# A perceiver layer on one core: the span attention's minimum taken a half batch later, and a product with the values moved within odd half batches

## The chip, the cores and the metric

The kernel runs on one core of a Trainium2 chip. The metric is the time of one execution on the device in microseconds, given as the median of several runs; one further execution was profiled, and what is said of engines, waits and single instructions comes from that one. A core has five engines that run side by side, each through its own list of instructions in a fixed order: TensorE (PE; matrix products and transposes, results in PSUM), VectorE (DVE), ScalarE (ACT), GpSimd (POOL) and SyncE (SP), which here issues most of the transfers (three early ones are ScalarE's). An engine waits at an instruction until the semaphores that the instruction names have been raised; everything behind it in its list waits too.

## What is computed

A perceiver layer in float32: cross attention from 64 latent rows to 1601 context rows for each of 32 batches, a self attention whose weights come from a learnt span, and a shared and a hashed mixture of feed-forward nets. Cut to what matters:

```python
x = x + xattn(layernorm(x), ctx, ctx)          # 16 heads of 16, 64 x 1601 scores a head
x = x + span_attention(layernorm(x))
x = x + ffn(layernorm(x))                      # shared silu net + two hashed experts

def span_attention(h):                         # per head: two numbers a row
    span, value = heads(h @ W_span.T), heads(h @ W_val.T)
    mean, soft = sigmoid(span[..., 0]) * m, softplus(span[..., 1])
    scores = -soft * (pos - mean) ** 2         # 64 x 64 per head
    return (softmax(scores) @ value) @ W_out.T
```

## The kernel before

**Half batches and stretches.** The main loop (L763) runs over 64 half batches: n = 2b + c, with b the batch and c the half of the heads. In step n it makes the scores of half batch n + 1, the softmax of n and the products with the values of n - 1, and it projects the context of batch b + 1: keys (`project_keys`, four pieces) and values (`project_values`, units 0 to 6 of two blocks of 124 rows each; units 0 to 2 in even steps, 3 to 6 in odd ones). A step has three stretches, one for each call of `scores`. The order on every engine is the order of the calls, written out by hand.

**One step, in TensorE's order (PE):** the first product with the values of n - 1 (`values(n - 1, 0)`, L633, into `pvs`); the scores of stretch 0 (L546, four PSUM tiles `psc`); the transposes `pm` of the row maxima of n (L594, they read `mx`); key piece 0; the transposes `pb` that spread the maxima back (L609); the span steps that are due (`run(3n)`); the second product `values(n - 1, 1)`; the scores of stretch 1 (L546, five blocks a row, so five `psc` tiles and a spare one); key piece 1; two value units; the steps of stretch 1; the scores of stretch 2; key pieces 2 and 3 and the rest of the value units, in four column tiles each (`tiled`); the steps of stretch 2.

**The other engines.** VectorE adds the mask to each score tile on its way to SBUF (`prob`, L570; the fifth blocks in L563), keeps a running maximum in PSUM (`mrun`, L587) and at the end of the step writes `mx`; the maxima after `pm` are reduced to `mc` (L601). ScalarE copies the projections out of PSUM (L507 keys, L524 values), copies the maxima `mb` (L613), begins a running maximum with a copy (L579) and does the softmax exponentials, four a step (L623). GpSimd subtracts the maxima from the scores, four times a step (L618). In even steps `finish_steps` on VectorE (L708 to L716) divides the products of the batch before by their sums.

**The span steps.** After every second batch, one tile t of 128 rows (two batches) is finished: the output projection of the cross attention and then the span attention, as a generator `span_steps` with 23 steps. A table says in which stretch, counted from the step in which the tile becomes ready (n = 4t + 4), each step runs: `STEPS` for tiles 0 to 12, and a table each for the last three. Since a tile takes four half batches, steps of two or three tiles are under way at a time. The steps, by the index of the table: 0 `po` (PE, L248), the residual add (DVE, L251) and the statistics; 1 and 2 the spread (POOL) and the normalisation (ACT, L214); 3 the transposes `tr_h` (PE) and the copy `hT` (ACT, L260); 4 `psp` (PE); 5 an exponential; 6 a chain of small VectorE operations (L291 to L303); 7 `pos - mean` (POOL, L308); 8 the square (ACT, L312) and the product with `soft` (POOL, L313); 9 the minimum `least` (DVE, L316); 10 to 13 four exponentials each (ACT, L320), which take `least` as their bias; 14 the reciprocal of the totals (DVE, L325); 15 the product with it (POOL, L327); 16 `pval` (PE, L336) and its copies to `vbd`; 17 the transposes `psa` (PE, L354) and copies `aT`; 18 to 22 the products `po` (L364 and L374), the second residual add (L377) with statistics, normalisation and the transposes `tr_f` whose copies (L387) feed the feed-forward nets. A second generator, `query_steps`, makes the queries of a later tile (`tr_q`, `xnT`, `pq`, `qbd`) from odd steps on.

**PSUM.** All of `psc`, `pk`, `pv`, `pm`, `pb`, `po`, `tr_h`, `psa` and the like take the next of six banks (`mm_bank`, tag `mm`); one more holds `pvs` with the spare score tile, and one `mrun`. A product into a bank waits until what the bank held has been read. So the order of the calls also settles which copy or add each product waits for.

**Wherever a step's list has several entries,** they run in the order in which they were put on the list: an entry goes there when its step before has run.

**The tail.** After the last step of the loop the last half batch is finished, the steps of the last tiles run in stretches 1 to 21 after `3 * last`, and between them stand the units of the shared feed-forward net (`unit`, `gate`; L662 on PE, L684 to L690 on ACT and DVE). Then come the experts (L905 on).

Of the kernel before, what the change touches and what calls it, by code (L numbers as in the profile page):

```python
# [18 lines left out]
ALU = mybir.AluOpType  # L19
# [70 lines left out]
def perceiver_kernel(ctx: ExitStack, tc: tile.TileContext, a: dict[str, bass.AP], out: bass.AP):  # L90
    nc = tc.nc
# [125 lines left out]
    def transposed(src, name: str):  # L217
# [10 lines left out]

    STEPS = (3, 4, 5, 6, 7, 8, 9, 10, 11, 12, 13, 14, 15, 16, 18, 19, 20, 21, 23, 24, 25, 26, 27)
    LAST_BUT_TWO = (
        3, 4, 5, 6, 7, 8, 9, 10, 11, 12, 12, 13, 14, 15, 16, 17, 17, 18, 20, 21, 22, 23, 24,
    )
    LAST_BUT_ONE = (2, 2, 3, 4, 5, 5, 6, 7, 8, 9, 10, 10, 10, 10, 11, 11, 12, 13, 14, 15, 15, 16, 17)
    LAST = (2, 2, 3, 4, 5, 6, 8, 9, 10, 11, 12, 12, 12, 12, 13, 13, 14, 15, 16, 17, 17, 18, 19)
    SMALL = 6

    def steps_of(t: int):
# [2 lines left out]
    def span_steps(t: int, oT):  # L242
        at = steps_of(t)
        waits = iter([b - a for a, b in zip(at, at[1:])])
# [61 lines left out]
        full = [P, H, S]  # L306
        sc = span_pool.tile(full, F32, tag="sc", name=f"sc_{t}")
# [7 lines left out]
        least, total = small("least"), small("total")  # L315
        nc.vector.tensor_reduce(least, sc, AX.X, ALU.min)  # L316
        yield next(waits)
        for part in range(4):
# [3 lines left out]
                    accum_out=total[:, h : h + 1],  # L322
                )
            yield next(waits)
        nc.vector.reciprocal(total, total)  # L325
        yield next(waits)
        nc.gpsimd.tensor_tensor(sc, sc, total[:, :, None].to_broadcast(full), ALU.mult)  # L327
        yield next(waits)


        pval = mm_bank(f"pval_{t}")
# [10 lines left out]
        for e in range(2):  # L342
            nc.scalar.copy(
                vbd[e * S : (e + 1) * S, :, e * DK : (e + 1) * DK],
                pval[e * S : (e + 1) * S, : 2 * P].rearrange("p (n d) -> p n d", d=DK),
            )
        yield next(waits)
        scf = sc.rearrange("p h k -> p (h k)")
        aT = span_pool.tile([P, NPAIR, P], F32, tag="aT", name=f"aT_{t}")
        for q in range(2):  # L350
            ps = mm_bank(f"psa_{t}_{q}")
            for i in range(4):
                n = 4 * q + i
# [175 lines left out]
    def scores(n: int, g: int, then=None, order=None):  # L529

        b, c = halves[n]
        c0, nb = SCORED[g]


        more = [mm_bank(f"psc_{b}_{c}_{g}"), spare_pvs] if nb == 5 else None
        pss = [mm_bank(f"psc_{b}_{c}_{g}_{j}") for j in range(4)]
        for r in range(nb):
            for j in range(4):
                e, s = divmod(j, 2)[::-1]
                fifth = nb == 5 and r == 4 * s  # L540
                i = 4 if fifth else r - (nb == 5 and s == 0)
                ps, at = (more[e], s) if fifth else (pss[j], i)
                if fifth and j == 2:
                    tc.add_manual_dep(nc.tensor.nop().ins, mm.ins.name, IN_TURN, reason="banks")
                k0 = (c0 + i) * CHUNK
                product = nc.tensor.matmul(  # L546
                    ps[:CHUNK, at * P : (at + 1) * P],
                    lhsT=kTs[c][32 * j : 32 * j + 32, k0 : k0 + CHUNK],
                    rhs=qbd[b // 2][32 * j : 32 * j + 32, c, b % 2, :, :],
                    start=True, stop=True, tile_position=(32 * j, 0),  # L550
                )
                if fifth and j == 1:
                    mm = product
        held = then() if then else None
        for item in (order or ORDER[g]).split():
            if item == "t":
                if held is not None:
                    maxima_of_rows(*held)
            elif item[0] == "m":
                maximum(n, int(item[1:]))  # L560
            elif item in "AB":
                k, e = c0 + 4, "AB".index(item)
                nc.vector.tensor_tensor(  # L563
                    block_of(n, k)[:, :, e, :],
                    more[e][:CHUNK, : 2 * P].rearrange("p (r q) -> p r q", r=2),
                    madd_fifth[:CHUNK, None, :].to_broadcast([CHUNK, 2, P]), ALU.add,
                )
            else:
                j = int(item)
                nc.vector.tensor_tensor(  # L570
                    pair_of(n, j)[:, c0 : c0 + 4, :].rearrange("p k (e q) -> p k e q", e=2),
                    pss[j][:CHUNK].rearrange("p (k e q) -> p k e q", k=4, e=2),
                    madd[:CHUNK, c0 : c0 + 4, None, :].to_broadcast([CHUNK, 4, 2, S]), ALU.add,
                )
# [3 lines left out]
    def first_maxima(n: int):  # L578
        nc.scalar.copy(mrun[:CHUNK].rearrange("p (r i) q -> p r i q", r=2), block_of(n, 0))  # L579
# [45 lines left out]
    def values(n: int, r: int):  # L625

        b, c = halves[n]
        v = vs[b % 2]
        for k in range(NKC):
            kn = min(CHUNK, KEYS - k * CHUNK)  # L630
            for j in range(4):
                h = 4 * r + j
                nc.tensor.matmul(  # L633
                    pvs[32 * j : 32 * j + DK + 1, c, :, r, :],
                    lhsT=v[:kn, k, 8 * c + h, :],
                    rhs=pair_of(n, h // 2)[:kn, k, (h % 2) * S : (h % 2) * S + S],
                    start=(k == 0), stop=(k == NKC - 1), tile_position=(0, 32 * j),
                )
# [56 lines left out]
    def run(stretch: int):  # L695
        for steps in agenda.pop(stretch, []):
            while (wait := next(steps, None)) == 0:
                pass
            if wait:
                agenda[stretch + wait].append(steps)  # L700

    def finish_steps(b: int, stretch: int):

        t = b // 2
        if b % 2 == 0:
            oT[t] = work.tile([P, 2, 2, S], F32, tag="oT", name=f"oT_{t}")
        flat = "p c u r q -> p (c u r q)"
        nc.vector.transpose(turned_pvs.rearrange(flat), pvs.rearrange(flat))  # L708
        by_head = turned_pvs.rearrange("p c u r i -> p (c u r) i")
        rec = work.tile([P, 8], F32, tag="rec", name=f"rec_{b}")  # L710
        nc.vector.reciprocal(rec, by_head[:, :, DK])
        o = work.tile([P, 8, DK], F32, tag="o", name=f"o_{b}")
        nc.vector.tensor_tensor(
            o, by_head[:, :, :DK], rec[:, :, None].to_broadcast([P, 8, DK]), ALU.mult
        )
        nc.vector.transpose(oT[t][:, :, b % 2, :], o.rearrange("p (c n) i -> p c (n i)", c=2))  # L716
        if b % 2:
            at = steps_of(t)
            agenda[stretch - 1 + at[0]].append(span_steps(t, oT.pop(t)))
            held_at.add(stretch - 1 + at[SMALL])  # L720
        yield
# [41 lines left out]
    for n, (b, c) in enumerate(halves[:-1]):  # L763
        if c == 0 and b + 1 < B:
            load_context(b + 1)
        if c and b % 2 == 0 and b // 2 + 1 < NTILE:
            agenda[3 * n].append(query_steps(b // 2 + 1))

        def project(f, *args):
            if b + 1 < B:  # L770
                f(b + 1, *args)

        def steps(g: int):
            run(3 * n + g)
            for u in extra.get(3 * n + g, ()):
                linear_factor(u)

        def taken_off():
            turned.extend(turned_maxima(n))
            return turned  # L780

        turned: list = []
        if n:
            values(n - 1, 0)
            exponentials(n - 1, 3)
        scores(n + 1, 0, taken_off)
        project(project_keys, c, 0)
        m = maxima_along_rows(turned[1])
        less_maxima(n, 0, m, nc.gpsimd)
        held = 3 * n in held_at  # L790
        if not held:
            first_maxima(n + 1)
        run(3 * n)
        if n:
            values(n - 1, 1)
            if c == 0:
                agenda[3 * n + 1].append(finish_steps(b - 1, 3 * n + 1))
        for u in extra.get(3 * n, ()):
            linear_factor(u)
        if held:  # L800
            first_maxima(n + 1)
        else:
            for k in (1, 2):
                maximum(n + 1, k)

        scores(n + 1, 1, order=LATER if held else None)
        exponentials(n, 0)
        project(project_keys, c, 1)
        for u in (4, 5) if c else (0, 1):
            project(project_values, u)  # L810
        less_maxima(n, 1, m, nc.gpsimd)
        steps(1)
        exponentials(n, 1)

        less_maxima(n, 2, m, nc.gpsimd)
        scores(n + 1, 2)
        project(project_keys, c, 2, True)
        project(project_keys, c, 3, True)
        for u in (3, 6) if c else (2,):
            project(project_values, u, True)  # L820
        less_maxima(n, 3, m, nc.gpsimd)
        exponentials(n, 2)
        steps(2)
# [176 lines left out]
```

## Time and profile before

| | |
|---|---|
| median of 3 runs | 1527.41 us (1525.89 to 1528.43) |
| the profiled execution: time, span | 1530.65 us, 1528.8 us |
| busy, share of the span: PE, DVE, ACT, POOL | 96%, 80%, 62%, 73% |
| granted TensorE clock, mean | 0.992 |
| mean DMA rate | 48 GB/s |
| `least` (L316), one | 1.10 to 1.19 us |
| an exponential of L320, one (x256) | 342 ns |
| L618 (GpSimd), one (x252) | 3753 ns |

Times in the lines of the profile are microseconds from the start of the span unless marked ns. A line of a timeline has the start, the time of the instruction or of several like it, the engine, the line of the code, the operation, what it writes and reads, and in brackets how long the engine stood idle before it and what ended that. A line of the chain of waits has the start, the time and the instruction; "issue" is time in which the profile shows nothing that was waited for. A PE that is busy is not a PE at its peak, since products are pipelined.

### The profile page before, as it was taken

What the parts mean: (1) busy time and instruction counts of PE and PEld (TensorE: products, weight loads), DVE (VectorE), ACT (ScalarE), POOL (GpSimd) and SP (SyncE); (2) the same over time, 40 slices, a digit from 0 to 9 for tenths busy, and PEclk for the clock granted to TensorE, in tenths of its full rate; (3) what the DMA queues carried; (4) which work ended last, traced back from release to release, by engine and by line L of the source; (5) the groups of instructions that cost most, each with busy time, mean ns of one, the idle gap of its engine ahead of it and who ended that gap; (6) DMA issues with size and microseconds to landing.
All of it is one profiled execution on the core that took longest, in us unless ns stands there. A gap on an engine that the chain in (4) does not pass through costs nothing.

```text
span 1528.8 us, 62985 instructions
## 1 busy us (share of the span) xinstructions
PE 1469.1 (96%) x28600; PEld 1069.2 (70%) x28600; DVE 1224.9 (80%) x2332; ACT 947.6 (62%) x1725; POOL 1121.4 (73%) x508
## 2 busy tenths in 40 slices
PE   8999999999999999999999999999999999988999
PEld 5677767677776767776767767676777777654587
DVE  4889898989888898989898888988898888873100
ACT  3565667666767666666757676666766676756311
POOL 1777788888787878888887878777888778852700
PEclk9999999999999999999999999999999999999899
DMA  5111111111111101111111111011111111005100
GB/s 173 44 37 46 46 46 46 50 38 49 49 49 50 45 25 40 53 46 44 44 50 49 50 49 46 23 42 53 37 51 46 49 46 36 3 6 159 59 28 28
DMA packets 52076, 73.82 MB, mean 48 GB/s; under 512 B 3812, under 2 KB 51040, under 8 KB 51680
## 3 DMA queue, kind: packets, MB, share of 16 engines
q1 hardware_dynamic: 50992, 69.00, 14.8%
q8 instruction: 225, 3.69, 1.0%
q10 hardware_dynamic: 816, 0.79, 0.2%
q14 instruction: 43, 0.35, 0.1%
HBM read 65.57 MB, written 4.19 MB: 46 GB/s over the span
## 4 chain that ended last, share of the span: by engine, by line
PE 77%; DVE 18%; ACT 2%; issue 2%; DMA 0%; POOL 0%; ACTq 0%; POOLq 0%; DVEq 0%
PE pk L492 20%; PE pv L492 18%; PE psc L546 11%; PE pvs L633 10%; DVE mrun L587 8%; DVE prob L570 5%; PE py L930 4%; PE pm L594 2%; PE u L662 2%; PE pb L609 2%; PE ph L912 2%; DVE least L316 1%; PE pq L463 1%; PE psa L354 1%; PE po L248 1%
## 5 line engine op out<-in xcount | busy, mean ns | idle before, releaser
L618 POOL TENSOR_TENSOR prob<-prob,mb 124x1664 f32<-124x1664 f32 x252 | 939.5, 3753 | 222.3 <-ACT mb L613 189.0
L570 DVE TENSOR_TENSOR prob<-psc,madd 124x512 f32<-124x512 f32 x768 | 506.2, 680 | 67.9 <-PE psc L546 66.7
L587 DVE TENSOR_TENSOR mrun<-prob,mrun 124x512 f32<-124x512 f32 x704 | 486.5, 691 | 28.3 <-ACT mrun L579 15.5
L623 ACT ACTIVATE prob<-prob 124x1664 f32<-124x1664 f32 x256 | 406.8, 1590 | 143.2 <-POOL prob L618 140.6
L492 PE MATMUL pk<-ct,wkT_sb 128*32 128x372 f32 (+1 forms) x2512 | 388.6, 490 | 5.6 <-DMA wkT_sb<-in_wkT 5.5
L492 PE MATMUL pv<-wvT_sb,ct 128*124 128x256 f32 x3524 | 380.9, 379 | 0.1
L492 PEld LDWEIGHTS pv<-wvT_sb,ct 128*124 128x124 f32 x3524 | 273.0, 132 | 108.8 <-issue 11.6
L546 PE MATMUL psc<-qbd,kT 32*124 32x128 f32 x6400 | 243.6, 280 | 10.7 <-issue 8.4
L492 PEld LDWEIGHTS pk<-ct,wkT_sb 128*32 128x32 f32 (+1 forms) x2512 | 149.2, 127 | 137.0 <-issue 92.7
L546 PEld LDWEIGHTS psc<-qbd,kT 32*124 32x124 f32 x6400 | 203.1, 181 | 49.1 <-issue 27.4
L524 ACT COPY v<-pv 124x512 f32<-124x512 f32 (+1 forms) x224 | 124.6, 557 | 181.9 <-PE pv L492 181.9
L633 PE MATMUL pvs<-prob,v 124*17 124x64 f32 x13312 | 212.7, 220 | 2.7 <-issue 2.7
L633 PEld LDWEIGHTS pvs<-prob,v 124*17 124x17 f32 x13312 | 195.4, 98 | 24.4 <-issue 16.5
L507 ACT ACTIVATE kT<-pk,cols 128x372 f32<-128x372 f32 (+2 forms) x256 | 148.0, 589 | 87.9 <-PE pk L492 87.7
L320 ACT ACTIVATE sc<-sc,least 128x64 f32<-128x64 f32 x256 | 85.8, 342 | 3.2 <-DVE least L316 3.2
L932 DVE SCALAR_TENSOR_TENSOR ot<-py,prob 128x256 f32<-128x256 f32 x16 | 6.8, 424 | 75.7 <-PE py L930 66.1
L594 PE MATMUL pm<-cst,mx 124*128 124x124 f32 x256 | 42.2, 285 | 22.7 <-DVE mx L587 18.9
L662 PE MATMUL u<-xfT,sw_sb 128*128 128x512 f32 x128 | 59.7, 615 | 0.9 <-ACT xfT L387 0.9
L579 ACT COPY mrun<-prob 124x512 f32<-124x512 f32 x64 | 38.4, 599 | 29.4 <-DVE soft L303 26.4
L546 PE MATMUL pvs<-qbd,kT 32*124 32x128 f32 x256 | 55.1, 294 | 0.0
L609 PEld LDWEIGHTS pb<-cst,mc 128*124 128x124 f32 x256 | 29.0, 135 | 37.3 <-DVE mc L601 29.0
L563 DVE TENSOR_TENSOR prob<-psc,madd_fifth 124x256 f32<-124x256 f32 x64 | 27.0, 422 | 32.2 <-PE pvs L546 29.1
(125 smaller groups left out, 1246.7 us busy)
## 6 DMA issues: line engine op xcount, KB each, us to landing
ct<-in_ctxT SPq DMA_DIRECT2D x64, 372.0 KB, 3.2
ct<-in_ctxT SPq DMA_DIRECT2D x32, 496.0 KB, 5.1
ct<-in_ctxT SPq DMA_DIRECT2D x32, 361.0 KB, 3.9
w<-in_w SPq DMA_DIRECT2D x16, 256.0 KB, 7.7
x<-in_x SPq DMA_DIRECT2D x16, 128.0 KB, 2.3
x_kept<-x SPq DMA_DIRECT2D x16, 128.0 KB, 2.3
prob<-x_kept SPq DMA_DIRECT2D x8, 256.0 KB, 5.3
out<-ot SPq DMA_DIRECT2D x16, 128.0 KB, 1.9
```

Of the source, the lines that this page charges most:

```text
L320: nc.scalar.activation(sc[:, h, :], sc[:, h, :], AF.Exp, bias=least[:, h : h + 1], scale=-1.0, accum_out=total[:, h : h + 1],)
L492: nc.tensor.matmul(out[at:end], lhsT=lhsT[:, at:end], rhs=rhs, start=start, stop=stop, **(dict(tile_position=(0, at)) if tiled else {}),)
L507: nc.scalar.activation(kTs[c][:, k0 : k0 + kn], ps[:, :kn], AF.Identity, bias=cols[:, B_K + c : B_K + c + 1])
L524: nc.scalar.copy(vs[b % 2][:kn, 2 * u : 2 * u + n, :, :DK], ps[:kn, : n * D].rearrange("p (n h d) -> p n h d", n=n, d=DK),)
L546: product = nc.tensor.matmul(ps[:CHUNK, at * P : (at + 1) * P], lhsT=kTs[c][32 * j : 32 * j + 32, k0 : k0 + CHUNK], rhs=qbd[b // 2][32 * j ...
L570: nc.vector.tensor_tensor(pair_of(n, j)[:, c0 : c0 + 4, :].rearrange("p k (e q) -> p k e q", e=2), pss[j][:CHUNK].rearrange("p (k e q) -> ...
L587: nc.vector.tensor_tensor(dst, block_of(n, k), run, ALU.max)
L594: nc.tensor.transpose(ps[:, j * CHUNK : (j + 1) * CHUNK], m[:CHUNK, j, :], ident[:CHUNK, :CHUNK])
L618: engine.tensor_tensor(sj, sj, m[:CHUNK, j, None, :].to_broadcast([CHUNK, NKC, P]), ALU.subtract)
L623: nc.scalar.activation(pair_of(n, j), pair_of(n, j), AF.Exp)
L633: nc.tensor.matmul(pvs[32 * j : 32 * j + DK + 1, c, :, r, :], lhsT=v[:kn, k, 8 * c + h, :], rhs=pair_of(n, h // 2)[:kn, k, (h % 2) * S : ( ...
L662: nc.tensor.matmul(ps, lhsT=w[:, c, hc * P : (hc + 1) * P], rhs=xfT[:, c, :, slot], start=(c == 0), stop=(c == 1),)
```

## The change

Three things change. The table `STEPS` puts the steps from 7 on later: `pos - mean` from 10 to 11, the square and product from 11 to 12, `least` from 12 to 15, the four groups of exponentials from 13 to 16 to 16 to 19; the tables of the last three tiles are changed too. In `span_steps` the step with `pval` now comes before the reciprocal and the product with it, which take its places 15 and 16 in the table. And in odd half batches value unit 3 is projected in stretch 0, ahead of the steps due there and in whole products instead of column tiles, while `values(n - 1, 1)` is moved from stretch 0 to stretch 2, after the scores there.

```diff
-    STEPS = (3, 4, 5, 6, 7, 8, 9, 10, 11, 12, 13, 14, 15, 16, 18, 19, 20, 21, 23, 24, 25, 26, 27)
+    STEPS = (3, 4, 5, 6, 7, 8, 9, 11, 12, 15, 16, 17, 18, 19, 20, 20, 21, 22, 23, 24, 25, 26, 27)
     LAST_BUT_TWO = (
-        3, 4, 5, 6, 7, 8, 9, 10, 11, 12, 12, 13, 14, 15, 16, 17, 17, 18, 20, 21, 22, 23, 24,
+        3, 4, 5, 6, 7, 8, 9, 11, 12, 13, 13, 14, 15, 16, 17, 17, 17, 18, 20, 21, 22, 25, 27,
     )
-    LAST_BUT_ONE = (2, 2, 3, 4, 5, 5, 6, 7, 8, 9, 10, 10, 10, 10, 11, 11, 12, 13, 14, 15, 15, 16, 17)
-    LAST = (2, 2, 3, 4, 5, 6, 8, 9, 10, 11, 12, 12, 12, 12, 13, 13, 14, 15, 16, 17, 17, 18, 19)
+    LAST_BUT_ONE = (
+        2, 2, 3, 4, 5, 5, 6, 7, 8, 9, 10, 11, 12, 13, 14, 14, 14, 15, 16, 17, 17, 18, 19,
+    )
+    LAST = (2, 2, 3, 4, 5, 6, 8, 9, 10, 11, 12, 12, 12, 12, 13, 13, 13, 15, 16, 17, 17, 18, 19)
...
             yield next(waits)
-        nc.vector.reciprocal(total, total)
-        yield next(waits)
-        nc.gpsimd.tensor_tensor(sc, sc, total[:, :, None].to_broadcast(full), ALU.mult)
-        yield next(waits)
         pval = mm_bank(f"pval_{t}")
...
         yield next(waits)
+        nc.vector.reciprocal(total, total)
+        yield next(waits)
+        nc.gpsimd.tensor_tensor(sc, sc, total[:, :, None].to_broadcast(full), ALU.mult)
+        yield next(waits)
...
         if not held:
             first_maxima(n + 1)
+        if c:
+            project(project_values, 3)
         run(3 * n)
-        if n:
+        if n and c == 0:
             values(n - 1, 1)
-            if c == 0:
-                agenda[3 * n + 1].append(finish_steps(b - 1, 3 * n + 1))
+            agenda[3 * n + 1].append(finish_steps(b - 1, 3 * n + 1))
...
         scores(n + 1, 2)
+        if c:
+            values(n - 1, 1)
         project(project_keys, c, 2, True)
         project(project_keys, c, 3, True)
-        for u in (3, 6) if c else (2,):
-            project(project_values, u, True)
+        project(project_values, 6 if c else 2, True)
```

## The prediction

> Half batches are q0, q1, q2, q3 by n mod 4 (c is odd in q1 and q3); V0 and V1 are the two products with the values, S0, S1, S2 the scores of the three stretches, line numbers those of the kernel before. I read the page's chain first, then the chain in detail over the four half batches from 785 to 870 us, then each engine's timeline there, and last the order and the semaphores of the changed kernel as built.
>
> **What bounds the kernel now.** The chain is TensorE's, with VectorE for 18% of the span:
>
> ```profile
> PE 77%; DVE 18%; ACT 2%; issue 2%; DMA 0%; POOL 0%; ACTq 0%; POOLq 0%; DVEq 0%
> ```
>
> In detail (start, us, what) it leaves TensorE once in four half batches, in q0:
>
> ```profile
> 789.38 0.43 DVE x L377
> ...
> 790.48 1.10 DVE least L316
> 791.58 0.61 DVE mrun L587
> ...
> 805.69 0.70 DVE mx L587
> 806.38 0.04 issue
> 806.43 0.64 PE pm L594 x4
> ```
>
> From the residual add at 789.38 VectorE never rests until mx, and TensorE's transposes pm of the next half batch (q1) wait for it. TensorE's timeline gives the wait:
>
> ```profile
> 806.43 0.64 PE L594 MATMUL pm<-cst,mx 124*128 124x124 f32 x4 [1.36 <-DVE mx L587]
> 829.37 0.38 PE L221 MATMUL tr_h<-cst,xn_h 128*128 128x128 f32 x2
> 829.90 1.65 PE L633 MATMUL pvs<-prob,v 124*17 124x64 f32 x104
> 831.47 0.37 PE L546 MATMUL psc<-qbd,kT 32*124 32x128 f32 x1
> ```
>
> In the steady part the q1, q2 and q3 half batches begin pm without such a wait; pm to pm they take 20.35, 21.05 and 20.59 us of TensorE alone, q0 20.70 with 1.36 of waiting. VectorE's and ScalarE's timelines show how much room the others have:
>
> ```profile
> 790.39 1.19 DVE L316 TENSOR_REDUCE least<-sc 128x16 f32<-128x1024 f32 x1
> 792.82 0.41 DVE L563 TENSOR_TENSOR prob<-psc,madd_fifth 124x256 f32<-124x256 f32 x1
> 810.08 0.42 DVE L251 TENSOR_TENSOR x<-x,po 128x256 f32<-128x256 f32 x1 [0.73 <-PE po L248]
> 813.19 0.42 DVE L563 TENSOR_TENSOR prob<-psc,madd_fifth 124x256 f32<-124x256 f32 x1 [0.16 <-PE pvs L546]
> 824.38 0.37 ACT L524 COPY v<-pv 113x256 f32<-113x256 f32 x1 [0.28 <-PE pv L492]
> 824.65 1.59 ACT L623 ACTIVATE prob<-prob 124x1664 f32<-124x1664 f32 x1
> 826.14 0.59 ACT L214 ACTIVATE xn_h<-x,neg_h,rstd_h 128x256 f32<-128x256 f32 x1
> 826.63 0.59 ACT L214 ACTIVATE xn_q<-x,neg_q,rstd_q 128x256 f32<-128x256 f32 x1
> 827.54 1.59 ACT L623 ACTIVATE prob<-prob 124x1664 f32<-124x1664 f32 x1 [0.32 <-POOL prob L618]
> 829.13 0.67 ACT L507 ACTIVATE kT<-pk,cols 128x496 f32<-128x496 f32 x1
> 830.69 0.38 ACT L260 COPY hT<-tr_h 128x256 f32<-128x256 f32 x1
> ```
>
> In q1 the first add of S1 (L563, 813.19) waits 0.16 for TensorE; ScalarE, from the last copy of q1's values (824.38) to hT (830.69) in q2, rests 0.32 only. hT matters: its bank is taken again by S1.
>
> **The change part by part.**
>
> *q0, least removed: -0.55.* Without 1.10 us of least the two maxima start at 790.48 and would free VectorE at 791.72 or so (1.32 from start to next start, as at 791.50 to 792.82). But the next operation, L563, needs S1 whole: in q1 it starts 1.42 after S1 does (811.77 to 813.19). S1 starts at 790.85 in q0, so L563 starts at 792.27, not 792.82. Nothing later in that chain waits, so mx and pm come 0.55 earlier and 0.81 of the 1.36 stays. Bounds: 0.3 to 0.81 of gain.
>
> *q1, least added, and the value projection 3 put ahead of run: +0.58.* The projection (1.73 us; two units are 3.45 in the chain, at 814.59 in q1) stands before po, so po starts 4.31 after pm and not 2.58. The x add starts 1.07 after po (809.01 to 810.08): 5.38. least comes ahead of it and fits into the wait, 2.45 us after the four score adds (809.35); it costs nothing, and would cost up to its 1.10 without that cover. From the x add, the two statistics and the two maxima take 2.86 (810.08, 811.62, plus 1.32), so L563 starts at pm + 8.24, before it was 6.76. S1's fifth-block bank is the one that the next value projection but one (unit 4) writes: it waits until L563 is done, 8.24 + 0.41 + 0.07 (from a copy's end to the waiting engine's start, 789.23 to 789.30 at mb) = 8.72; before, it started at 7.99. That is 0.73; 0.15 is the projection's excess over the V1 (1.58) that left this place and is given back later. Left: 0.58. A shorter wait of about 0.35 (S1's sixth product needs the bank of po) lies inside it. From L563 to the end of mx are 12.39 (813.19 to 825.73, less a rest of 0.15), so mx ends at pm + 20.63, and TensorE arrives at 20.35 + 0.58 = 20.93: no second wait. Bounds 0.3 and 0.75.
>
> *q2, the exponentials: +1.69.* least in q1 shifts its four groups of exponentials (four each, L320) from q0's and q1's stretches to q1's stretches 1 and 2 and q2's 0 and 1. In the built order the second group stands in ScalarE's queue before xn_h, xn_q and the softmax exponential 3 of q1, and the third right before hT. So 8 x 0.335 = 2.68 us (a group is 1.34: 818.56 to 819.90) come between two points that had 0.32 to spare. ScalarE's path from the last value copy on, each from its start to the next start: copy 0.27, exponential 2 1.49, group 1.34, xn twice 1.00, exponential 3 1.50, kT 0.57, mb 0.47, first maxima 0.52, group 1.34, hT 0.38: 8.88. TensorE's path from the same copy to S1's sixth product, whose bank is hT's: 831.47 - 824.38 + 0.10 = 7.19. S1 waits 1.69 for it. Queued behind hT are xnT (the next bank) and exponential 0; behind the stalled S1 is all of q2. SP's queue is not moved past, and no DMA is added. Bounds: 1.2 (exponential 3's own 0.32 wait and V1's wait on it overlapping) and 1.9.
>
> *Cover that I cost at nothing.* V1 to the last stretch of q1 and q3: TensorE does the same work, the tiled projection (2.59 for three blocks) being as long as the plain one (3.45 for four); pair and values buffers stay unwritten until then. q0: L313 (1.90) now follows POOL's first subtraction, so the third ends about 1.48 after pm instead of 0.93 before it; exponential 3 and mb come 0.6 later, still ahead of what q1 waits for. q2's POOL loses L327, q3's gets it (exponential 1 at 861.0 had 2.2 us of room), q3's psa moves a stretch later at equal length. The tables of the last three tiles move the same steps by a stretch in half batches 60 to 62 (the last two 23.27 and 23.41 long): nothing, within 2 either way. The fourth group comes before qbd in q2; the key projection that waits for it (by some 0.3) starts later too.
>
> [...]
>
> *Tail: -1.* Tile 14's exponentials split over four stretches no longer stand in one block of 5.4 us (1373.23 to 1378.55) ahead of xn_f, for which TensorE rests 6.89. The last tile's po moves from 1384 to about 1376, but its later steps meet two more table loads of 1.28 each, five units of 1.72 and the later steps of tile 14. By the rows its Square moves from 1404.54 to 1403.5. Bounds: -5 (the rest gained nearly whole) and +3.
>
> [...]
>
> *Sum.* q0: 13 tiles on the main table x -0.55 = -7.2. q1: 14 x 0.58 = +8.1 (15 half batches from n = 5, without n = 61, which has other waits). q2: 13 x 1.69 = +22.0. Tail -1. Together +21.9 against the profiled 1528.8; the profiled run as a whole is 1530.65, 3.2 above the median 1527.41, so I add the difference to the median: 1549.3.
>
> **The rivals.**
> 1. *Faster: only VectorE's wait changes.* If the exponentials lie in ScalarE's rests and the banks come free in time, q0's gain stands alone: 1527.4 - 7.2 - 1 = 1519, and with all of the 1.36 13 x 1.36 = 17.7, 1509. For it: ScalarE is busy 62%, least is on the chain. Against: its rests are elsewhere (0.32 in this stretch). It decides once the path of 8.88 is really under 7.19. Chance 0.10.
> 2. *Nothing: the copy hT is not what S1 waits for.* -7.2 + 8.1 - 1: 1527. Against: the built waits name it. Chance 0.06.
> 3. *Worse: the delay is handed on.* The fourth group delays qbd, exponential 1 and so the next V0, or VectorE ends late in q2 as well: another 0.5 to 1 in 13 cycles, +6 to +13: 1556 to 1562. Against: after the wait TensorE is later by 1.69 and the others have this room. Chance 0.12.
> The forecast has 0.72.
>
> **How the numbers follow.** All low ends together (q0 0.81, q1 0.3, q2 1.2, tail -5): -10.5 + 4.2 + 15.6 - 5 = +4.3; all high ends: -3.9 + 10.5 + 24.7 + 3 = +34. The forecast's own range is therefore 1532 to 1562. Cut to 1531 to 1560 it keeps nearly all of the forecast and more than half of rival 3. What can be told from no change is some 0.2% (3 us). Faster 0.10 (rival 1), same 0.06 (rival 2), slower 0.84.
>
> **What would show it.** The wait before pm in q1 falls to about 0.8; in q1 a wait of 0.3 to 0.7 appears at S1 and the value projection; in q2 S1 shows 1.2 to 1.9 waiting for hT (L262 there); q1's length is about 20.9, q2's 22.7, q0's 20.15, q3's 20.6. I am wrong if q2 stays at 21.05, or if pm at q2 waits for mx.

## The result, and the profile after

The changed kernel takes 1536.68 us (median of 4, 1535.58 to 1539.09), the kernel before 1526.77 us beside it (median of 4): ratio 1.0063, 95% interval 1.0049 to 1.0078. It is slower, by 9.9 us; the forecast was slower by 21.9. The profiled execution after took 1539.09 us with a span of 1537.3, 8.5 more than the 1528.8 before. Line numbers below are those of the kernel named; up to L237 they are the same in both, from there the changed kernel's are some 2 higher (L594 is L596, L587 is L589, L260 is L262, L320 is L322).

First the chain of the changed kernel, by engine:

```profile
PE 71%; DVE 20%; ACT 6%; issue 2%; POOL 0%; DMA 0%; DVEq 0%; ACTq 0%; POOLq 0%
```

ScalarE has gone from 2% to 6%: a new engine has come onto the path, as forecast. TensorE's timeline of the changed kernel, q1 and q2 of the same tile as the rows of before, shows where:

```profile
814.14 0.64 PE L596 MATMUL pm<-cst,mx 124*128 124x124 f32 x4 [0.81 <-DVE mx L589]
822.84 3.72 PE L494 MATMUL pv<-wvT_sb,ct 128*124 128x256 f32 x16 [0.26 <-DVE prob L565]
835.02 0.64 PE L596 MATMUL pm<-cst,mx 124*128 124x124 f32 x4
839.88 0.37 PE L548 MATMUL psc<-qbd,kT 32*124 32x128 f32 x1
841.45 1.03 PE L548 MATMUL psc<-qbd,kT 32*124 32x128 f32 x26 [0.88 <-ACT hT L262]
```

The three waits stand where the prediction put them: 0.81 of the old 1.36 is left before q1's pm; q1's value projection, 8.70 after pm, waits for the score add L565; and in q2 the bulk of S1 waits for hT. The bracket of the last one says 0.88, since the ten products of the trace before it (two for each of S1's first five) still count as busy. What the wait costs is read from the starts: 841.45 is 6.43 after pm, while before it was 4.92 (826.78 to 831.70), so 1.51 is lost. The chain of waits of the changed kernel between those points (start, us, what):

```profile
832.62 0.06 ACT v L526
...
832.88 1.60 ACT prob L625
834.48 1.32 ACT sc L322 x8
835.80 0.49 ACT xn_h L214
836.29 0.49 ACT xn_q L214
836.78 1.04 ACT prob L625
...
838.72 0.57 ACT mb L615
839.29 0.48 ACT mrun L581
839.77 1.37 ACT sc L322 x8
841.15 0.26 ACT hT L262
841.41 0.04 issue
841.45 1.03 PE psc L548 x26
```

From the value copy at 832.62 ScalarE has no rest before hT is written. The two groups of L322, 1.32 and 1.37, are the ones the new table put there; without them the path of 8.83 (832.62 to 841.45) would be 6.14, well inside TensorE's 7.32.

So the waits came as forecast, and the change in time was still less than half of the forecast one (the 1536.68 lies near the low end of the range of 1531 to 1560). The half batches say why. In each kernel one length from pm to pm stands out for each kind, the same to within a few hundredths of a microsecond: before, 9 of 11 half batches of q0 and all 12 of q1 have it, but only 4 of 12 of q2 and 2 of 12 of q3. Most of the others are 0.1 to 2 us longer, a few of q2 shorter. I call this length the undisturbed one and sum what the others have above it, over the 47 half batches n = 13 to 59 (11 of q0, 12 of each other):

| n = 13 to 59 | q0 | q1 | q2 | q3 | stage, us |
|---|---|---|---|---|---|
| undisturbed, before | 20.70 | 20.35 | 21.05 | 20.59 | |
| undisturbed, after | 20.15 | 20.88 | 22.57 | 20.45 | |
| difference x count | -6.0 | +6.4 | +18.2 | -1.7 | +16.9 |
| above undisturbed, before | 3.4 | 0.1 | 5.9 | 10.8 | 20.2 |
| above undisturbed, after | 0.2 | 4.1 | 0.4 | 7.7 | 12.4 |
| stage: 991.8 before, 1000.9 after | | | | | +9.05 |

The undisturbed lengths grew by 16.9, near the forecast. But 7.8 came back in the "above undisturbed" rows, of which the prediction said nothing. The two profiled executions lie 3.9 and 2.4 above the medians; from the medians' 9.9 the same sum gives about 6.5 (an estimate: 16.9 - 0.5, for what lies outside these half batches, - 9.9). Behind most of it are pauses of TensorE with no releaser, in the waits of the kernel before over its whole span (engine, line, waited for: us, times, longest):

```profile
PE psc L546 <- issue: 8.4, 12, 1.6
PE pm L594 <- issue: 3.1, 4, 1.7
PE pvs L633 <- issue: 2.7, 5, 0.9
```

The clearest row is q2's. In it TensorE rests 3.05 us in such pauses before, and q2 is 5.94 above its undisturbed length; after, it rests 4.29, yet q2 is only 0.43 above. The pauses are still there, but S1 would have waited for hT anyway, and where they fall ahead of it they lie under that wait. Two like pauses just ahead of S1 show it, n = 14 before and n = 18 after (TensorE's timelines):

```profile
327.00 0.22 PE L633 MATMUL pvs<-prob,v 113*17 113x64 f32 x1 [0.89 <-issue]
```

```profile
413.63 0.52 PE L635 MATMUL pvs<-prob,v 124*17 124x64 f32 x21 [0.94 <-issue]
```

The first makes its half batch 1.10 longer than the undisturbed one, the second makes it no longer (22.57). The wait takes in pauses from q1 too: the q2 half batches that are shorter than undisturbed after the change, n = 26, 34, 42 and 50 by 0.18 to 0.79, are the four that follow a q1 half batch with a pause. q2 alone gives back 5.5 of the 7.8. The other 2.3 lie elsewhere (q0 -3.3, q1 +4.1, q3 -3.1); 1.5 of q0's are a stretch at half clock before, shown in the last section, which the trace after does not have.

Outside these half batches: up to the first pm +0.9, n = 0 to 12 +1.1, n = 60 to 62 +0.6, from the last pm to the experts -3.1. Together -0.5, and 9.05 - 0.5 is the 8.5 of the spans. In the tail the wait for tile 14's last normalised rows is shorter, 3.15 in place of 6.89, in TensorE's timeline of the changed kernel:

```profile
1413.23 0.44 PE L221 MATMUL tr_f<-cst,xn_f 128*128 128x128 f32 x2 [3.15 <-ACT xn_f L214]
```

### The profile page after: what moved, and what is told of

The parts are those of the page before. It is cut to its first block, busy times and chain, and to the rows that moved or that the text cites. A ratio compares the mean times of both kernels' runs of the same rounds, so it can differ in the third digit from the quotient of the medians.

```text
span 1537.3 us, 61465 instructions
## 1 busy us (share of the span) xinstructions
PE 1472.5 (96%) x27856; PEld 1085.6 (71%) x27856; DVE 1222.5 (80%) x2332; ACT 953.3 (62%) x1727; POOL 1118.5 (73%) x508
## 4 chain that ended last, share of the span: by engine, by line
PE 71%; DVE 20%; ACT 6%; issue 2%; POOL 0%; DMA 0%; DVEq 0%; ACTq 0%; POOLq 0%
PE pv L494 18%; PE pk L494 17%; PE psc L548 10%; PE pvs L635 9%; DVE mrun L589 8%; DVE prob L572 6%; PE py L934 4%; ACT sc L322 2%; PE pm L596 2%; PE u L664 2%; PE ph L916 2%; PE pb L611 2%; ACT prob L625 1%; DVE prob L565 1%; PE pq L465 1%
## 5 line engine op out<-in xcount | busy, mean ns | idle before, releaser
L589 DVE TENSOR_TENSOR mrun<-prob,mrun 124x512 f32<-124x512 f32 x704 | 486.2, 691 | 38.6 <-ACT mrun L581 25.9
L494 PE MATMUL pv<-wvT_sb,ct 128*32 128x256 f32 (+1 forms) x2780 | 387.4, 380 | 4.8 <-DVE prob L565 4.4
L494 PEld LDWEIGHTS pv<-wvT_sb,ct 128*32 128x32 f32 (+1 forms) x2780 | 284.9, 145 | 101.3 <-issue 14.1
L548 PE MATMUL psc<-qbd,kT 32*124 32x128 f32 x6400 | 249.0, 281 | 16.4 <-issue 7.6
L548 PEld LDWEIGHTS psc<-qbd,kT 32*124 32x124 f32 x6400 | 207.7, 181 | 57.4 <-issue 29.7
L635 PEld LDWEIGHTS pvs<-prob,v 124*17 124x17 f32 x13312 | 196.7, 98 | 27.3 <-issue 16.5
L322 ACT ACTIVATE sc<-sc,least 128x64 f32<-128x64 f32 x256 | 85.7, 339 | 2.8 <-DVE least L318 2.8
L596 PE MATMUL pm<-cst,mx 124*128 124x124 f32 x256 | 41.2, 283 | 15.7 <-DVE mx L589 14.4
L565 DVE TENSOR_TENSOR prob<-psc,madd_fifth 124x256 f32<-124x256 f32 x64 | 26.9, 421 | 31.1 <-PE pvs L548 31.1
```

The lines of the kernel that those rows point to most:

```text
L322: nc.scalar.activation(sc[:, h, :], sc[:, h, :], AF.Exp, bias=least[:, h : h + 1], scale=-1.0, accum_out=total[:, h : h + 1],)
L494: nc.tensor.matmul(out[at:end], lhsT=lhsT[:, at:end], rhs=rhs, start=start, stop=stop, **(dict(tile_position=(0, at)) if tiled else {}),)
L548: product = nc.tensor.matmul(ps[:CHUNK, at * P : (at + 1) * P], lhsT=kTs[c][32 * j : 32 * j + 32, k0 : k0 + CHUNK], rhs=qbd[b // 2][32 * j ...
L589: nc.vector.tensor_tensor(dst, block_of(n, k), run, ALU.max)
L596: nc.tensor.transpose(ps[:, j * CHUNK : (j + 1) * CHUNK], m[:CHUNK, j, :], ident[:CHUNK, :CHUNK])
L635: nc.tensor.matmul(pvs[32 * j : 32 * j + DK + 1, c, :, r, :], lhsT=v[:kn, k, 8 * c + h, :], rhs=pair_of(n, h // 2)[:kn, k, (h % 2) * S : ( ...
```

## The experiments

Each kernel ran beside the kernel before on its chip (medians 1525.01 and 1525.48 there); ratios are against that. "Stage" is n = 13 to 59 as above; a negative "above" means that half batches were shorter than the undisturbed length.

| kernel | us | ratio, 95% | q0 | q1 | q2 | q3 | above | stage |
|---|---|---|---|---|---|---|---|---|
| before | | | 20.70 | 20.35 | 21.05 | 20.59 | 20.2 | 991.8 |
| after | 1536.68 | 1.0063 (1.0049-1.0078) | 20.15 | 20.88 | 22.57 | 20.45 | 12.4 | 1000.9 |
| e1_hT_first | 1521.95 | 0.9981 (0.9971-0.9991) | 20.15 | 20.88 | 21.25 | 20.45 | 13.5 | 986.1 |
| e4_unit3_after_run | 1523.61 | 0.9989 (0.9979-0.9998) | 20.15 | 20.22 | 22.57 | 20.45 | 6.9 | 987.4 |
| e5_both | 1512.46 | 0.9913 (0.9899-0.9928) | 20.15 | 20.22 | 21.25 | 20.45 | 12.7 | 977.4 |
| e2_tables_alone | 1528.68 | 1.0012 (1.0000-1.0024) | 20.15 | 20.35 | 22.57 | 20.59 | 7.2 | 990.9 |
| e3_product_alone | 1529.69 | 1.0030 (1.0017-1.0042) | 20.70 | 20.88 | 21.05 | 20.59 | 14.3 | 992.3 |

**e1: hT ahead of the exponentials.** In q2's stretch 0 the list of steps has the exponentials first and hT's after them; this turns them round, with the same work on every engine.

```diff
-        for steps in agenda.pop(stretch, []):
+        due = agenda.pop(stretch, [])
+        if stretch % 12 == 6:
+            due = due[1:] + due[:1]
+        for steps in due:
```

> The changed kernel with one edit: in the first stretch of the half batches with n mod 4 = 2 (q2) the oldest entry of the list (the third group of four exponentials) runs last, so ScalarE copies hT and xnT before it. My theory (ScalarE's queue ahead of hT holds S1 in q2): that queue shrinks by one group of 1.34 us, so the wait falls from about 1.5 to 0.2 and q2 from 22.57 to about 21.3 from pm to pm; 13 half batches x 1.25 = 16 us, so 1521 us if TensorE's other pauses stay as they are. The addition I make now (pauses that TensorE makes without any named releaser, before the change some 20 us over half batches 13 to 59 and after it 12, lie under the new waits and come back when these go): 1523 to 1529 us. Rival (q2 is longer for another reason, such as POOL being late): 1535 to 1539 us, q2 still near 22.5.

1521.95, a little below the 1523 to 1529 that were expected. q2 falls from 22.57 to 21.25, nothing else changes its length, and in its timeline S1 runs on without a bracket:

```profile
830.95 0.47 PE L548 MATMUL psc<-qbd,kT 32*124 32x128 f32 x3
831.15 0.27 PE L548 MATMUL pvs<-qbd,kT 32*124 32x128 f32 x1
831.16 1.06 PE L548 MATMUL psc<-qbd,kT 32*124 32x128 f32 x29
```

So it is the place of the group in ScalarE's queue, not its work, that costs q2. And the cover is lifted with the wait: q2 rests less in pauses than after (2.47 against 4.29), but stands 4.4 above its undisturbed length again.

**e4: value unit 3 behind run(3n)**, so that po and the residual add come first, as before.

```diff
-        if c:
-            project(project_values, 3)
         run(3 * n)
+        if c:
+            project(project_values, 3)
```

> The changed kernel with value unit 3 of odd half batches projected after the span steps due in stretch 0 instead of ahead of them, so that po, tr_f, tr_h and tr_q come 1.73 us earlier. My theory (in q1 VectorE's x add waits for po, and the late maxima then hold the bank of the fifth blocks): q1 falls from 20.88 to about 20.35 from pm to pm and the wait of the value projection at pm + 8.7 goes; 14 x 0.53 = 7.4 us, so 1529 us, q2 unchanged at 22.57. Rival (least itself, now in q1, makes VectorE late): q1 stays near 20.9 and 1536 to 1538 us.

1523.61, where 1529 was expected. The value projection's bracket is gone, and so is all of the q1 term (20.88 to 20.22). TensorE's timeline of this kernel, q1:

```profile
807.07 1.03 PE L250 MATMUL po<-woP_sb,oT 128*128 128x256 f32 x4
807.93 0.38 PE L221 MATMUL tr_f<-cst,xn_f 128*128 128x128 f32 x2
808.15 1.89 PE L494 MATMUL pv<-wvT_sb,ct 128*124 128x256 f32 x8
...
812.63 2.54 PE L494 MATMUL pv<-wvT_sb,ct 128*124 128x256 f32 x11
```

The stage gains 13.5 us where the length explains 0.66 x 12 = 7.9: the pauses fell from 12.4 to 6.9 as well. The hT wait is still there, and q2 is even 1.2 shorter in sum than undisturbed. I read that so: where a pause in q1 makes TensorE late, ScalarE is nearer to hT when S1 comes. The half batches bear it out: the shorter ones are again n = 26, 34, 42 and 50 (by 0.18 to 0.79), and q1 paused in n = 25, 33, 41 and 49 alone.

**e5: both edits of e1 and e4.**

> Both edits together, unit 3 after the steps and hT first. Theory of two separate waits: the gains add, 16 + 7.4 us, so 1513 us with TensorE's unnamed pauses unchanged, 1515 to 1523 us if some come back; q0 20.15, q1 20.35, q2 21.3, q3 20.45 where no pause falls. It would then be faster than the kernel before (1526.8) by what is left of q0's gain and the tail's. Rival (one of the two only hands its wait to the next): no faster than the better one of the two alone.

1512.46, below the 1515 to 1523 expected with some pauses back, and the fastest kernel here: 0.9913 (0.9899 to 0.9928) of the one before. Both waits are gone, and the chain is again TensorE's, by engine:

```profile
PE 78%; DVE 18%; ACT 2%; issue 1%; POOL 0%; DMA 0%; ACTq 0%; DVEq 0%; POOLq 0%
```

Against e4 q2 loses 1.32 x 12 = 15.8 of length, and the stage only 10.0: the pauses go from 6.9 to 12.7, of which q2 takes 6.3 (-1.2 to 5.1). The same give and take as in the change itself, the other way round.

**e2 and e3: the two parts of the change alone.** e2 is the changed kernel with the product order of before; e3 the kernel before with the new product order and the old tables. e3's edit, whose reverse makes e2:

```diff
+        if c:
+            project(project_values, 3)
         run(3 * n)
-        if n:
+        if n and c == 0:
             values(n - 1, 1)
...
         scores(n + 1, 2)
+        if c:
+            values(n - 1, 1)
...
-        for u in (3, 6) if c else (2,):
-            project(project_values, u, True)
+        project(project_values, 6 if c else 2, True)
```

> The changed kernel with the product and value unit 3 put back where they were before (so the tables and the order of the span steps alone change). Theory of the waits: q0 keeps 20.15, q1 loses its wait and has 20.35 (least fits into VectorE's rest), q2 keeps the wait for hT at about 22.5, q3 20.59: against before 13 x (-0.55 + 1.5) = +12 less 3 in the tail, 1535 us with TensorE's pauses unchanged, 1529 to 1533 us if the wait covers some. Rival (the tables need the move of the product, because exponential 3 is late for it in stretch 0 of q1): q1 over 21, 1540 us or more.

> The kernel before with the move of the second product and of value unit 3 alone; tables and order of the span steps stay. Theory of the waits: q0 keeps its 1.36 (20.70), q1 gets its wait at the value projection (20.88, as VectorE's x add comes 1.73 us later whether least is there or not), q2 stays at 21.05, q3 becomes 20.45: 14 x 0.53 - 13 x 0.14 = +5.6 us on the lengths without a pause. Theory of the pauses (TensorE pauses where a block of its instruction stream ends within a dense run of small products; V1 no longer stands in front of S1 and unit 3 has 24 records fewer): the excess over those lengths in half batches 13 to 59, 20 us before, falls to some 13 us, so 1522 to 1527 us in all. Rival (q1's wait comes from least): q1 20.35, and 1518 to 1525 us.

The lengths come apart cleanly. The tables alone give q0's gain and q2's loss; the product alone gives q1's loss, although `least` is still in q0 there. TensorE's timeline of e3, q1:

```profile
816.60 3.72 PE L492 MATMUL pv<-wvT_sb,ct 128*124 128x256 f32 x16 [0.26 <-DVE prob L563]
```

So q1's wait comes from the unit ahead of po and not from the move of `least`. The tail belongs to the tables: 77.5 in e2, 82.2 in e3, against 82.1 before. The times do not come apart: e2's lengths make +12.2 in the stage, and it is 3.7 slower than the kernel before; its pauses are 7.2 and not 20.2. (Its profiled execution, 1525.06, is the quickest of its ten.) The profiled execution of the kernel before, 1530.65, is above all 25 runs of that kernel beside e2 (1522.40 to 1530.27), so the gap between 20.2 and 7.2 can be in part one between executions. e3 was expected faster or equal and is 4.2 slower: q3 did not get its 0.14. In the traces its pauses fall by 5.9 and nearly pay for q1's 6.4 (stage 992.3 against 991.8); by the medians they do not.

**e7: one group of exponentials more ahead of hT**, a dose of the suspected cost.

```diff
-    STEPS = (3, 4, 5, 6, 7, 8, 9, 11, 12, 15, 16, 17, 18, 19, 20, 20, 21, 22, 23, 24, 25, 26, 27)
+    STEPS = (3, 4, 5, 6, 7, 8, 9, 11, 12, 15, 16, 17, 18, 18, 20, 20, 21, 22, 23, 24, 25, 26, 27)
```

> The changed kernel with two of the four groups of exponentials ahead of hT in q2 instead of one (the table has 16, 17, 18, 18): the suspected cause doubled. Theory of ScalarE's queue: q2 becomes longer by one group, 22.57 + 1.34 = 23.9 us from pm to pm, the other three unchanged; 13 x 1.34 = 17 us less what it covers of pauses: 1547 to 1553 us. Rival (q2's length is set by something else, as POOL or the exponentials of the softmax): q2 under 23.2, 1534 to 1542 us.

1563.84, ratio 1.0254 (1.0234 to 1.0274), well above what was expected. In three half batches (n = 18, 30 and 58) q2 is 23.89, which is 22.57 and one group, 1.33: the price was right. But six others take 25.55 to 26.78. The timeline of e7 has the same wait in both kinds, n = 18 first, n = 46 second:

```profile
421.70 1.03 PE L548 MATMUL psc<-qbd,kT 32*124 32x128 f32 x26 [2.20 <-ACT hT L262]
...
422.78 1.52 PE L494 MATMUL pk<-ct,wkT_sb 128*128 128x372 f32 x4
...
1030.12 1.03 PE L548 MATMUL psc<-qbd,kT 32*124 32x128 f32 x26 [2.20 <-ACT hT L262]
...
1031.20 2.35 PE L494 MATMUL pk<-ct,wkT_sb 128*128 128x372 f32 x4
```

The same key projection takes 1.52 and 2.35. Windows of e7 behind the two waits (window, us, busy and count of PE, PEld, DVE, ACT, POOL, then the granted clock, the DMA share and GB/s):

```profile
421.70:424.70 3.00, 3.00 (x37) 2.32 (x38) 1.81 (x4) 2.17 (x3) 3.00 (x2) 1.00 0.00 0
424.70:429.70 5.00, 5.00 (x51) 4.48 (x53) 4.83 (x12) 1.95 (x5) 5.00 (x3) 1.00 0.00 0
1030.12:1033.12 3.00, 3.00 (x34) 2.13 (x35) 1.81 (x4) 1.81 (x2) 3.00 (x2) 0.77 0.00 0
1033.12:1038.12 5.00, 5.00 (x22) 4.04 (x20) 3.92 (x7) 1.38 (x3) 5.00 (x3) 0.80 0.01 3
```

The clock is the second price. The missing 0.23 of 3 us and 0.20 of 5 make 1.7 us of lost clock, or 3.4 us at half speed; n = 46 is 2.1 longer than n = 18. In the whole loop of e7 the trace has eight times 3.41 us at half clock, in the main stage of the changed kernel none; at 1.7 each they make some 13.7 us (an estimate), about as much as the time lies above what was expected.

**e6: what the pauses are.** Between two pauses of the kernel before, the number of TensorE's instructions (products and weight loads) is a multiple of 256 to within 1: 1536, 2049, 1536, 3584, 2815, 1025, 2560 for the first seven between 300 and 1300 us, that is 6, 8, 6, 14, 11, 4 and 10 times 256. More than that: counted from TensorE's first instruction of the trace (as 0), the instruction behind each releaserless rest of 0.15 us or more in n = 13 to 59 is number 193 or 194 modulo 256, for 127 rests of 127, in all ten kernels. And a packet of 16,384 bytes in the instruction queue (q8 in the page) starts 2.2 to 2.9 us before the end of each of the 17 rests of the kernel before. The reading: TensorE's stream comes in blocks of 256 instructions, and a pause is a block that arrives late. Then instructions put in at the start must move the pauses to other products, and a whole block must move them back. Each product put in here is two products and two loads in the trace: 32 of them are 128 instructions, half a block, and 64 a whole one.

```diff
+    zeros = const.tile([P, P], F32, name="zeros")
+    nc.vector.memset(zeros, 0.0)
+    for _ in range(32):
+        nc.tensor.matmul(
+            mrun[:, 0, :32], lhsT=zeros, rhs=zeros[:, :32], start=True, stop=True
+        )
```

> The kernel before with 32 small products (64 records of the profile) ahead of the first key projection, where TensorE waits for a load anyway; nothing else. Theory of the pauses (16 KB blocks of TensorE's instruction stream, about 127 records each): the block ends move by half a block, so the pauses of 0.2 to 1.7 us fall into other half batches than before (not n = 14, 18, 24, 35, 39, 47 again), still multiples of 127 records apart, and their sum in half batches 13 to 59 changes from 20 us to anything between 8 and 30: the time moves by more than 2 us from that before, either way. Rival (pauses belong to operations or places): the same half batches, 1524 to 1528 us.

> The kernel before with 64 small products (128 records) ahead of the first key projection: a whole block. Theory of the pauses: the block ends fall where they fell before, within two or three records, so the pauses come in the same half batches as before (n = 14, 18, 24, 27, 35, 39, 47, 55) with a sum of 17 to 23 us in half batches 13 to 59, and the time is that of before plus what the products add at the start: 1525 to 1529 us. Rival (any shift of the stream scatters them): other half batches, another sum.

What single half batches have above their undisturbed length, us:

| n | 14 | 23 | 24 | 34 | 35 | 39 | 43 | 47 | 51 | 58 |
|---|---|---|---|---|---|---|---|---|---|---|
| before | 1.10 | 0 | 1.90 | 0 | 1.44 | 1.25 | 1.38 | 2.03 | 0 | 0 |
| half a block more | 0.13 | 1.04 | 0 | 0.70 | 1.96 | 0 | 0.73 | 0.82 | 1.12 | 0.89 |
| a whole block more | 1.37 | 0 | 1.33 | 0 | 1.71 | 0.90 | 1.41 | 1.58 | 0 | 0 |

Half a block brings pauses to n = 23, 34, 51 and 58 and takes them from 24 and 39; a whole one undoes all of that. n = 35, 43 and 47 keep one in all three kernels, against what was expected, but at another product: in n = 35 it ends 7.01 us after pm before, 22.14 with half a block more and 7.28 with a whole one. The totals are 16.5 and 16.5 (17 to 23 was expected of the second), against 20.2. The times, 1531.61 and 1547.95, say little of the pauses, and the second was missed: the products put in cost 9.7 and 23.6 us before the first pm, more than I had allowed, and the whole excess of the second kernel lies there.

Most block ends cost nothing that the trace shows: the main stage before has some 163 of them (41,712 instructions by 256; 163 packets start in the instruction queue in it) and 17 rests of 0.15 us or more without a releaser. But these rests sum to 11.4 us, more than half of the 20.2.

## Why the prediction was wrong

**Right.** That the change slows the kernel, and through what. q0: -0.55, to the hundredth, with 0.81 of the wait left. q1: the wait for L563's add, +0.53 against +0.58; e3 and e4 show its cause, the unit ahead of po. q2: the copy hT behind the group of exponentials; e1 and e7 show that both its place and its dose decide. No second wait at pm followed in any of them, so rival 3 fell with rivals 1 and 2.

**The step that failed is the sum,** "q2: 13 x 1.69 = +22.0", and under it the sentence "they take 20.35, 21.05 and 20.59 us of TensorE alone". Those are the lengths of half batches without a pause. In the trace of before q2 took 21.55 in the mean and q3 21.49, and that was there to be read. A delay of 1.51 in a half batch in which TensorE has already lost time, in it ahead of the same point or at the end of the one before, adds only the difference. The sum took the pauses as unchanged, without a word: that is the term it put at nothing. On n = 13 to 59, the prediction's prices by these counts against what was measured:

| term | predicted | measured |
|---|---|---|
| q0, x 11 | -6.0 | -6.0 |
| q1, x 12 | +7.0 | +6.4 |
| q2, x 12 | +20.3 | +18.2 |
| q3, x 12 | 0 | -1.7 |
| pauses | not in the sum | -7.8 |
| sum | +21.2 | +9.05 |

Of the 12.2 between the sums the pauses are 7.8 and the sizes 4.4. That a wait hides pauses is shown three times: q2 loses its 5.5 in the change, gets 3.9 back in e1, and 6.3 from e4 to e5. That they are blocks that arrive late is a reading; it rests on the place modulo 256, the packets and e6. Where they fall in a new kernel none of my expectations worked out beforehand, and e2's total of 7.2 is not explained.

**Sizes.** q2's 1.69 was 1.52: ScalarE's path was 8.83 (predicted 8.88) and TensorE's 7.32 (predicted 7.19). The tail gave -3.1 and not -1, inside its bounds of -5 and +3.

**V1's new place, taken at nothing.** Something was gained here, and no run shows the reason. With V1 away from its place in q1 and unit 3 behind run, q1 is 20.22 against 20.35 (e4 and e5), and q3 is 20.45 against 20.59 in the changed kernel: 0.13 and 0.14, or 3.2 us over 24 half batches. The timelines place it, from start to next start: V1 takes 1.58 at its old place, behind tr_f, psa or pb alike, and 1.47 behind S2; the key pieces behind S2 take 2.49 before and 2.46 where V1 stands between. The 0.09 that the transposes gain ahead of a plain projection (0.31 to 0.22) is lost again by unit 3 ahead of S1 (1.73 to 1.82). Where S1 stands directly behind transposes of the span steps, with no product between, it takes 1.44 and not 1.30: in q1 after the change (the prediction had a short wait of about 0.35 at this point) and in e3's q3 behind psa. So e3's q3 keeps 20.59 because this 0.14 takes the gain back, and e2's because V1 has not moved.

## What to carry to other kernels

Add a new wait to the undisturbed length of a stage, but set the sum against the mean length of before, not against the best one: idle time that the profile puts on no releaser is room that a wait further on can fill where it falls ahead of that wait, and it comes back when the wait is mended. When work is moved to a step list shared with a copy that TensorE waits for, ask which of the two stands first in the engine's queue. Here the change as made lost 0.6%, and with two entries turned round, or one projection put behind po, it gains 0.2% or 0.1%, with both 0.9%.

## What was not expected of the hardware

**Half clock behind waits of 2.2 us.** In e7 the eight half batches whose wait for hT is a full 2.20 are alike up to the wait; five of them then run 3.4 us at half clock and three do not. So does n = 10 behind a bracket of 1.78, and n = 26 runs 6.8 us so behind one of 0.73 and a pause of 1.06 just ahead of it; with the brackets of 0.88 of the changed kernel and e4 none of the main stage does. The slow stretches in e7's loop begin 26, 51, 25, 77, 51 and 51 times 3.413 us apart (94, 5, 11 and 33 times over the whole trace of the kernel before; 7, 5 and 36 times in the changed kernel's). Why five of the eight waits of 2.20 have one behind them and three have none is not shown. In the kernel before a slow stretch followed one of the 17 pauses (timeline, then the window in the columns above):

```profile
1040.23 0.64 PE L546 MATMUL psc<-qbd,kT 32*124 32x128 f32 x9 [1.61 <-issue]
1040.80 1.09 PE L594 MATMUL pm<-cst,mx 124*128 124x124 f32 x4
1041.68 2.93 PE L492 MATMUL pk<-ct,wkT_sb 128*128 128x496 f32 x4
```

```profile
1040.46:1043.87 3.41, 3.41 (x16) 2.01 (x12) 2.94 (x5) 0.03 (x1) 0.53 (x1) 0.50 0.02 5
```

The transposes take 1.09 and not 0.64, the projection 2.93 and not 1.83: 1.5 of the 20.2 us above undisturbed are this one stretch.

**Small products into one bank.** The products put in by e6 (128x128 by 128x32) take 13.87 us for 32 and 27.51 for 64, so 0.43 each. The first pm comes 9.7 and 23.6 later, less than that, since the first key projection waited 5.48 for its load before.
